# A gated transformer block on one core: the order of DMAs in an attention unit, and four smaller moves

## The chip, the cores and the metric

The kernel runs on one core of one Trainium2 chip. The metric is device time in microseconds (us) of one execution. Times of the kernel before are of three runs; the profile is of one more execution.

The engines are named as the profile names them: PE (TensorE, matmuls), DVE (VectorE), ACT (ScalarE), POOL (GpSimd) and SP (SyncE), which here only issues DMAs, in order, one queue for all of them.

## The reference, cut to what matters

The input `x` is 8 blocks of 128 rows by 512. Four layers are added to it, each behind a normalisation and times the tanh of a gate:

```
x = x + tanh(g_xattn[0]) * attention(layernorm(x), ctx, mask, position_bias, wq, wk, wv, w_out)
x = x + tanh(g_ffn[0])   * (layernorm(x) @ W4bit + f0_bias)
x = x + tanh(g_xattn[1]) * attention_one_head(layernorm(x), ctx, ...)
x = x + tanh(g_ffn[1])   * (layernorm(x) @ base_W.T + base_b + routed low-rank experts)
```

The first attention takes most of the time: 32 heads of 128, each over 8 blocks of 128 queries by 128 keys, with a bias for each head that all blocks share, a mask for each block, a softmax, the product with the values, and the output weights `w_out`, 128 rows of them for each head.

## The kernel before, in words

**Precision.** A product of two f32 matrices is done as three matmuls of high and low parts: each operand is split into a rounded part (`high`, by ACT) and the rest (`low`, by DVE or POOL), and the products high·high, high·low and low·high are summed in PSUM (`product`, L171, lines L177 to L179).

**Keys and queries (0 to some 310 us).** For a pair of heads, the 2x2 blocks of weights and context go through a scheme of seven products instead of eight (`seven`, L210). The first two pairs of keys are done plainly (`project_plainly`, L553): four PSUM banks, one for each head i and each half of the blocks, each summed over four row blocks of the context (two values of `inner`, two of `dc`). At the very start, SP loads the weights of head 0 (`wk_0`) and two blocks of the context, the weights of head 1 (`wk_1`) and two more, and then the other four blocks (L370 to L377). Keys and queries are stored to DRAM.

**Attention units (some 310 to 790 us).** A unit is one head and one half of the blocks; there are 64 (`unit`, L1005). In unit u of pair p, with r = u mod 4, are traced: two output products of a pair done before (`project_out`, L753, added into x on DVE by L750), value products (`make_values`, the next ones needed), the attention product `av` of unit u-4 (`attend`, L719), the sum of mask and position bias on POOL (`add_masks`, L651, instruction L657), the scores of unit u on PE (L669), their sum with mask and bias on DVE (L670), the negative maximum (L674), the transpose of the probabilities of unit u-3 on DVE (`transpose_probs`, L716, held behind that maximum), the exponentials on ACT (L684), and the normalising multiply on POOL (L692).

**The way through DRAM.** To transpose the probabilities, a unit stores them (`store_probs`, L700, tile `through`) and the next unit reads them back with four DMAs of 64 KB, each another block of 32 partitions (`move_probs`, L707, tile `moved`, two buffers). DVE then transposes within 32x32 blocks (L716, into `pT`), and PE uses `pT` in `av` (L731). One unit's chain is: scores, sum, maximum, exponentials, multiply, store, read, transpose, `av`.

**Loads of a unit.** `loads(u + 1)` (L992) is traced in unit u behind the store: queries and keys of unit u+4 (`fetch`, L580, DMAs L593), in two units of eight two blocks of value weights (`load_quad`, L281, tile `raw_wv`), the position bias of the next pair when the next unit has r = 3 (`load_bias`, L365), and a head's output weights when the next unit has r = 0 or 1 (`load_wo`, L281, tile `raw_wo`). The output weights are split into `wo_h` (ACT) and `wo_l` (POOL) in the units with r = 2 and 3 (`split_wo`, L354).

**What sets the order.** The program is traced in the order of the code; a planner then orders each engine's instructions by its own estimate of when each is ready, with earlier traced ones first. `behind(name)` (L139) holds what is traced within it behind a marked instruction on the same engine, without a semaphore. In the key and query stage and in the ending, PE keeps the traced order (`in_order`, L146); in the units the planner orders PE, too. Buffers are rotating slots with tags (L35): 4 of tag `s` (the scores of a unit, 256 KB), one of which the tile `cols` of small statistics holds (L736); 6 of tag `kq`, 7 of `raw`, 8 of `wo`.

**Ending (some 784 us on).** `ending` (L1338) does the last units' products, interleaved with the three later layers over the 8 blocks (`ffn0`, `xattn1`, `ffn1`). Before it, DVE multiplies the two biases of the later layers by their gates (L1067 into `bias0`, L1068 into `bb`); `add_row` (L1114) adds them to x on POOL.

Of the kernel before, what the change touches and what calls it, by code (L numbers as in the profile page):

```python
# [14 lines left out]
ALU = mybir.AluOpType  # L15
AX = mybir.AxisListType

P = 128
NB = 8
D = 512  # L20
NDC = D // P
H = 32
# [43 lines left out]
def kernel(  # L66
# [37 lines left out]
    nc = tc.nc  # L104
# [9 lines left out]
    def slot(shape, tag, name, dtype=F32):  # L114
        return sb.tile(shape, dtype, tag=tag, name=name, bufs=TAGS[tag])
# [6 lines left out]
    def wide_row(tag, name, dtype=F32):  # L122
        return slot([P, D], tag, name, dtype)
# [4 lines left out]
    def wide(t):  # L128

        return t.bitcast(F32)  # L130
# [4 lines left out]
    def mark(name, inst):  # L135
        marks[name] = inst.ins

    @contextmanager
    def behind(*names):  # L139
        with ExitStack() as stack:  # L140
            for name in names:
                stack.enter_context(tc.issue_after(marks[name]))
            yield
# [27 lines left out]
    def product(out, terms, start=True, stop=True, **more):  # L171


        n = len(terms)
        for i, ((lh, ll), (rh, rl)) in enumerate(terms):
            first, last = start and i == 0, stop and i == n - 1
            nc.tensor.matmul(out, lhsT=lh, rhs=rh, start=first, stop=False, **more)  # L177
            nc.tensor.matmul(out, lhsT=lh, rhs=rl, start=False, stop=False, **more)  # L178
            nc.tensor.matmul(out, lhsT=ll, rhs=rh, start=False, stop=last, **more)  # L179
# [6 lines left out]
    HK = NDC // 2  # L186
# [92 lines left out]
    def load(key, src, shape=(P, D)):  # L279
        t = slot(list(shape), "raw", f"raw_{key}")  # L280
        mark("load", nc.sync.dma_start(out=t, in_=src))  # L281
        raws[key] = t

    def load_pair(kind, p):
        if p < NP:
            w = {"wk": wk, "wq": wq}[kind]
            for h in (2 * p, 2 * p + 1):
                load(f"{kind}_{h}", w[:, h])
# [61 lines left out]
    def load_wo(h):  # L350
        if h < H:
            load(f"wo_{h}", wo[:, h])

    def split_wo(h):  # L354
        t = raws.pop(f"wo_{h}")
        high, low = (wide_row("wo", f"wo_{n}{h}", F32R) for n in "hl")
        split(high, low, t, nc.gpsimd)
        wos[h] = high, low
# [10 lines left out]
    cx_raw = {}  # L369
    for inner in range(2):  # L370
        for half in range(2):
            if inner == 0:
                load(f"wk_{half}", wk[:, half])
            for dc in range(inner * HK, inner * HK + HK):
                t = wide_row("wo", f"cxraw{half}{dc}")
                nc.sync.dma_start(out=t, in_=ctxT[:, dc, half * HALF * P : (half + 1) * HALF * P])
                cx_raw[half, dc] = t  # L377
    load_pair("wk", 1)
    lnw = wide_row("pT", "lnw")
    nc.sync.dma_start(out=lnw, in_=ln_w.partition_broadcast(P))  # L380
# [21 lines left out]
    tgx0, tgx1, tgf0, tgf1 = (tg[:, i : i + 1] for i in range(4))  # L402
# [150 lines left out]
    def project_plainly(kind, p, left, right):  # L553

        banks = {}

        turns = [(inner, half, i) for inner in range(2) for half in range(2) for i in range(2)]
        if p:
            turns.sort(key=lambda turn: (turn[1], turn[2], turn[0]))
        for inner, half, i in turns:  # L560
            if inner == 0:
                tag = ("mm", "av")[half]
                banks[i, half] = ptile([P, HALF * P], tag, f"c{i}{half}_{kind[0]}{p}")
            w, t = left[i], right[f"B{inner + 1}{half + 1}"]
            terms = [
                (
                    tuple(part[:, bass.ts(2 * inner + dc, P)] for part in w),
                    (t[:, 0, dc, :], t[:, 1, dc, :]),
                )
                for dc in range(HK)  # L570
            ]
            product(banks[i, half], terms, inner == 0, inner == 1)
            if inner:
                t = slot([P, HALF * P], "kq", f"{kind}{i}{half}_{p}")
                mark("copy", nc.scalar.copy(t, banks[i, half]))
                nc.sync.dma_start(out=stored[kind, p][:, 2 * i + half], in_=t)
# [126 lines left out]
    def move_probs(u):  # L703
        moved = slot([P, NQ, HALF, Q32], "moved", f"moved_{u}")
        blocks = probs[u].rearrange("(i q) n f -> n q i f", q=Q32)
        for j in range(NQ):
            move = nc.sync.dma_start(  # L707
                out=moved[bass.ts(j, Q32)].rearrange("p i b k -> p i (b k)"), in_=blocks[j]
            )
        mark("moved", move)  # L710
        probs[u] = moved
# [7 lines left out]
    def attend(u):  # L719
        h, half = where(u)  # L720
        p, i = divmod(h, 2)
        pT = probs.pop(u)
        if i == 0:
            attns[p, half] = page([P, 2, 2, HALF, P], f"a_{p}_{half}")
        a = attns[p, half][:, i]
        ah, al = a[:, 0], a[:, 1]
        cols = bass.ts(i, P)
        av = ptile([P, HALF, P], "av", f"av_{u}")
        for b in range(HALF):
            v = values_of[p, half, b // 2][:, b % 2, :]  # L730
            nc.tensor.matmul(av[:, b, :], lhsT=v[:, cols], rhs=pT[:, b, :], start=True, stop=True)  # L731
        mark("a", nc.scalar.copy(ah, av))  # L732
        mark("al", nc.vector.tensor_tensor(al, av, wide(ah), ALU.subtract))  # L733


    cols_all = slot([P, NB, 60], "s", "cols")  # L736
    places = {}

    def col(name, b, n=1):
        if name not in places:  # L740
            places[name] = sum(m for _, m in places.values()), n
        at, n = places[name]
        assert at + n <= 60
        return cols_all[:, b, at : at + n]

    def add_to_x(b, ps, factor, then=None):

# [151 lines left out]
    left = whole_pair(0)  # L899
# [61 lines left out]

    with in_order(*ORD):
        keys_and_queries()
    load_wo(0)

    last_keys = project(*order[-1], left, of_context)

# [24 lines left out]
    def loads(u):  # L992

        p, r = divmod(u, 4)
        n = u + (3 if u > FIRST - 4 else NU)
        if n >= FIRST:
            fetch(n)
        if u % 8 in (QUAD, QUAD + 1) and (u - QUAD) // 8 + 2 <= H // 4:
            load_quad((u - QUAD) // 8 + 2, (u % 8 - QUAD,))
        if r == 3:  # L1000
            load_bias(p + 1)
        if r in (0, 1):
            load_wo(2 * p + r)

    def unit(u):  # L1005
        p, r = divmod(u, 4)

        n = 2 * (u - OUT_LAG)

        goal = 14 + int(1.74 * (u - 3)) + min(AHEAD, u - 3, NU - 1 - u) if u > 3 else 0  # L1010
        if n >= 0:
            project_out(*divmod(n, NB))
        make_values((made + goal + 1) // 2)
        if u >= LAG:
            attend(u - LAG)
        if n >= 0:
            project_out(*divmod(n + 1, NB))
        make_values(goal)
        s = add_masks(u)
        for _ in range({0: 2, 1: 2, 2: 1, 3: 1, 4: 1}.get(u, 0)):  # L1020
            next(last_keys)
        scores(u, s)
        if u == NU - 1:
            move_probs(u - 1)
        store_probs(u)
        with behind("through"):
            loads(u + 1)
            if 0 < u < NU - 1:
                move_probs(u - 1)
        if r in (2, 3):  # L1030
            with behind("exp"):
                split_wo(2 * p + r - 2)

    make_values(7)
    unit(0)
# [18 lines left out]
    bias0 = load_row("bias0", f0_bias)  # L1054
    bq = load_row("bq", bq1)
    bb = load_row("bb", base_b)
# [6 lines left out]

    qkn = keep([P, NDC], "qkn")
    nc.vector.tensor_tensor(qkn, qnw, knw, ALU.mult)

    nc.vector.tensor_scalar(bias0, bias0, tgf0, None, ALU.mult)  # L1067
    nc.vector.tensor_scalar(bb, bb, tgf1, None, ALU.mult)  # L1068

    def transposed(b, name, src):  # L1070
        tag = "sc" if b % 2 and name in SC_NAMES else "av"
        tp = ptile([P, NDC, P], tag, f"tp{name}_{b}")
# [265 lines left out]
    def ending():  # L1338

        outs = iter(range(2 * (NU - OUT_LAG), NP * NB))  # L1340

        def project(n):
            for _ in range(n):
                project_out(*divmod(next(outs), NB))

        move_probs(NU - 1)
        with behind("moved"):
            for i in range(2):
                w_ffn.extend(load_page(f"wf{i}", ffn_kept[i]))
        make_values(made + 2)  # L1350
        project(2)
        attend(NU - 4)
        with behind("x"):
            transpose_probs(NU - 3)
        project(2)
        attend(NU - 3)
        project(1)
        yield
        project(3)
        with behind("x"):  # L1360
            transpose_probs(NU - 2)
        make_values(14 * (H // 4 + 1) - 2)
        attend(NU - 2)
        yield
        make_values(14 * (H // 4 + 1))
        transpose_probs(NU - 1)
        yield
        attend(NU - 1)
        project(4)
        yield  # L1370

    key, ffn, att, last = ([s(b) for b in range(NB)] for s in (keys, ffn0, xattn1, ffn1))
# [80 lines left out]
```

## Time and profile before

| what | us |
|---|---|
| median of three runs | 936.08 (935.97 to 937.21) |
| the profiled execution | 934.47 |
| its span | 932.7 |
| PE busy in it | 916.9 |
| DVE, ACT, POOL busy | 672.7, 503.4, 459.7 |

The span runs from the first to the last instruction of the program; the rest of the time lies around it. A busy PE is not PE at its peak, since the ends of matmuls are modelled; where PE loses time, its matmuls start further apart. Matmuls of 512 columns start some 0.23 us apart at full speed.

Issues by the page, with the median time to landing:

```profile
through<-s SPq DMA_DIRECT2D x64, 256.0 KB, 3.5
moved<-through SPq DMA_DIRECT2D x256, 64.0 KB, 3.8
q<-queries SPq DMA_DIRECT2D x58, 256.0 KB, 4.1
k<-keys SPq DMA_DIRECT2D x58, 256.0 KB, 4.8
```

A line gives the tile written and read, the queue, the count, the size of one, and the median us from issue to landing. In the answer on DMAs, those of `raw_wv` take 5.0 us, of `raw_wo` 5.1 and of the position bias 4.9.

### The profile page before, as it was taken

The numbers are of one execution on the slowest core, as the hardware profiler recorded it, in microseconds if no ns is written. First come the engines' busy times: TensorE is split into PE (matmuls) and PEld (weight loads), VectorE is DVE, ScalarE is ACT, GpSimd is POOL, SyncE is SP. The second block draws the span as 40 slices with busy tenths as digits, with TensorE's granted clock in tenths as the row PEclk, the third lists the DMA queues.
The fourth block names the chain that finished last, engine by engine and source line by source line (L and its number), as shares of the span: only waits on it lengthen the run. The fifth ranks groups of instructions, "written<-read, shape, count | busy, mean of one in ns | idle before, by whom it ended". The sixth has DMA issues, their size and how long they took to land.

```text
span 932.7 us, 16561 instructions
## 1 busy us (share of the span) xinstructions
PE 916.9 (98%) x5458; PEld 805.5 (86%) x5458; DVE 672.7 (72%) x1349; ACT 503.4 (54%) x1432; POOL 459.7 (49%) x513
## 2 busy tenths in 40 slices
PE   9999999999999998999999999999999999999998
PEld 7788888888888897999998889999998987888897
DVE  7887687888889676667676576766667667465686
ACT  6665465666645465445444444454545444577861
POOL 2455543133413445837567375673758733183441
PEclk9999999999999999999999999999999999999999
DMA  8665477889856928666665766666757566532001
GB/s 282 204 178 162 152 208 242 285 289 289 263 203 219 338 88 249 179 186 181 179 203 147 212 193 174 203 175 197 200 153 216 158 191 203 227 107 79 1 24 69
DMA packets 123909, 175.00 MB, mean 188 GB/s; under 512 B 16942, under 2 KB 52782, under 8 KB 122670
## 3 DMA queue, kind: packets, MB, share of 16 engines
q1 hardware_dynamic: 123822, 173.93, 61.5%
q8 instruction: 43, 0.70, 0.3%
q14 instruction: 44, 0.36, 0.1%
HBM read 109.85 MB, written 64.03 MB: 186 GB/s over the span
## 4 chain that ended last, share of the span: by engine, by line
PE 78%; DMA 7%; DVE 4%; ACT 4%; POOL 4%; issue 2%; SPq 2%; DVEq 0%; POOLq 0%; ACTq 0%
PE c_k L177 5%; PE pso L179 5%; PE c_k L178 5%; PE c_k L179 5%; PE pso L177 5%; PE c_q L177 5%; PE c_q L178 5%; PE c_q L179 5%; PE pso L178 5%; PE av L731 5%; PE c_v L177 5%; PE c_v L179 5%; PE c_v L178 5%; PE sc L669 4%; DMA moved<-through 3%
## 5 line engine op out<-in xcount | busy, mean ns | idle before, releaser
L684 ACT ACTIVATE s<-s,nm 128x128 f32<-128x128 f32 x256 | 99.8, 392 | 85.8 <-DVE nm L674 54.0
L750 DVE SCALAR_TENSOR_TENSOR x<-pso,tg,x 128x512 f32<-128x512 f32 x128 | 93.9, 738 | 47.5 <-PE pso L179 46.9
L692 POOL TENSOR_TENSOR s<-s,rs 128x512 f32<-128x512 f32 x64 | 66.8, 1044 | 85.9 <-DVE rs L690 65.6
L657 POOL TENSOR_TENSOR s<-mneg,bias 128x512 f32<-128x512 bf16 x64 | 75.8, 1190 | 65.8 <-DMA bias<-in_pbias_dram 23.9
L177 PE MATMUL pso<-wo_h,a 128*128 128x512 f32 x256 | 105.3, 413 | 1.2 <-DVE x L750 1.2
L179 PE MATMUL pso<-wo_h,a 128*128 128x512 f32 x256 | 105.6, 413 | 0.1
L178 PE MATMUL pso<-wo_l,a 128*128 128x512 f32 x256 | 101.1, 396 | 0.0
L732 ACT CAST a<-av 128x512 fp32r<-128x512 f32 x64 | 37.5, 585 | 96.0 <-PE av L731 96.0
L177 PE MATMUL c_v<-wvP,cxT 128*128 128x256 f32 x288 | 84.9, 295 | 0.6 <-ACT v L249 0.4
L179 PE MATMUL c_v<-wvP,cxT 128*128 128x256 f32 x288 | 81.4, 283 | 0.0
L178 PE MATMUL c_v<-wvP,cxT 128*128 128x256 f32 x288 | 81.3, 282 | 0.0
L731 PE MATMUL av<-pT,v 128*128 128x128 f32 x512 | 73.7, 278 | 5.4 <-DVE pT L716 5.4
L731 PEld LDWEIGHTS av<-pT,v 128*128 128x128 f32 x512 | 69.1, 192 | 10.8 <-DVE pT L716 6.6
L716 DVE STREAM_TRANSPOSE pT<-moved 128x512 f32<-128x512 f32 x64 | 45.0, 704 | 37.5 <-DMA moved<-through 37.5
L669 PEld LDWEIGHTS sc<-k,q 128*128 128x128 f32 x464 | 60.3, 191 | 4.9 <-DVE s L670 0.6
L669 PE MATMUL sc<-k,q 128*128 128x128 f32 x464 | 62.7, 275 | 0.4 <-DMA k<-keys 0.4
L177 PE MATMUL c_v<-wvP,cxB 128*128 128x256 f32 x216 | 62.0, 288 | 0.4 <-ACT v L264 0.4
L178 PE MATMUL c_v<-wvP,cxB 128*128 128x256 f32 x216 | 61.0, 282 | 0.0
L179 PE MATMUL c_v<-wvP,cxB 128*128 128x256 f32 x216 | 60.8, 282 | 0.0
L179 PEld LDWEIGHTS pso<-wo_h,a 128*128 128x128 f32 x256 | 48.6, 190 | 10.3 <-DVE a L733 1.3
L177 PEld LDWEIGHTS c_v<-wvP,cxT 128*128 128x128 f32 x288 | 54.8, 190 | 2.4 <-ACT wvP L168 0.7
L178 PEld LDWEIGHTS c_v<-wvP,cxT 128*128 128x128 f32 x288 | 54.8, 190 | 1.5
(281 smaller groups left out, 2801.2 us busy)
## 6 DMA issues: line engine op xcount, KB each, us to landing
keys<-keys SPq DMA_DIRECT2D x64, 256.0 KB, 3.6
queries<-queries SPq DMA_DIRECT2D x64, 256.0 KB, 3.7
through<-s SPq DMA_DIRECT2D x64, 256.0 KB, 3.5
moved<-through SPq DMA_DIRECT2D x256, 64.0 KB, 3.8
q<-queries SPq DMA_DIRECT2D x58, 256.0 KB, 4.1
k<-keys SPq DMA_DIRECT2D x58, 256.0 KB, 4.8
raw_wk<-in_wk_dram SPq DMA_DIRECT2D x32, 256.0 KB, 4.0
raw_wq<-in_wq_dram SPq DMA_DIRECT2D x32, 256.0 KB, 4.2
```

What stands on the lines that cost most here:

```text
L177: nc.tensor.matmul(out, lhsT=lh, rhs=rh, start=first, stop=False, **more)
L178: nc.tensor.matmul(out, lhsT=lh, rhs=rl, start=False, stop=False, **more)
L179: nc.tensor.matmul(out, lhsT=ll, rhs=rh, start=False, stop=last, **more)
L657: nc.gpsimd.tensor_tensor(s, mneg[:, half], bias.unsqueeze(2).to_broadcast([P, NQ, HALF, Q32]), ALU.add)
L669: nc.tensor.matmul(ps[:, j, :], lhsT=q[:, cols], rhs=k[:, cols], start=True, stop=True)
L684: e = nc.scalar.activation(one, one, AF.Exp, bias=nm[:, j : j + 1], accum_out=sm[:, j : j + 1])
L692: mark(f"norm{u}", nc.gpsimd.tensor_tensor(s, s, factors, ALU.mult))
L716: nc.vector.transpose(by_block(t), probs[u])
L731: nc.tensor.matmul(av[:, b, :], lhsT=v[:, cols], rhs=pT[:, b, :], start=True, stop=True)
L732: mark("a", nc.scalar.copy(ah, av))
L750: "x", nc.vector.scalar_tensor_tensor(xs[b], ps, factor, xs[b], ALU.mult, ALU.add, **out)
```

## The change

Five edits:

1. In a unit, the reads of the unit before (`move_probs`) come right behind the store, and the loads behind the reads (`behind("moved")`). Before, both were behind the store, the loads traced first.
2. The output weights of a pair are loaded one to two units later relative to their use (next unit r = 2 and 3 instead of 0 and 1 of the pair; the first one no longer ahead of the units) and split in the units with r = 3 and, of the next pair, r = 0. The last head's are split at the start of `ending`.
3. The tile `cols` is made when it is first used, in the ending, so that the units have four buffers of tag `s`.
4. The two gated biases are multiplied on DVE in the ending, behind `al` of unit 62.
5. The first two pairs of heads: for pair 0, the four banks are filled by one row block of the context at a time (both heads, then the next row block) and `wk_1` is loaded behind the first block instead of the second; in both pairs the three products of a term come in the order high·high, low·high, high·low, the low part of the weights first.

```diff
@@ loads at the start
-            if inner == 0:
-                load(f"wk_{half}", wk[:, half])
             for dc in range(inner * HK, inner * HK + HK):
+                if dc == half == 0:
+                    load("wk_0", wk[:, 0])
                 t = wide_row("wo", f"cxraw{half}{dc}")
                 nc.sync.dma_start(out=t, in_=ctxT[:, dc, half * HALF * P : (half + 1) * HALF * P])
                 cx_raw[half, dc] = t
+                if dc == half == 0:
+                    load("wk_1", wk[:, 1])
@@ project_plainly
-        turns = [(inner, half, i) for inner in range(2) for half in range(2) for i in range(2)]
+        turns = [
+            (*divmod(dc, HK), half, i)
+            for inner in range(2)
+            for half in range(2)
+            for dc in range(inner * HK, inner * HK + HK)
+            for i in range(2)
+        ]
         if p:
-            turns.sort(key=lambda turn: (turn[1], turn[2], turn[0]))
+            turns.sort(key=lambda turn: (turn[2], turn[3], turn[:2]))
...
+            nc.tensor.matmul(ps, lhsT=wh, rhs=th, start=first, stop=False)
+            nc.tensor.matmul(ps, lhsT=wl, rhs=th, start=False, stop=False)
+            nc.tensor.matmul(ps, lhsT=wh, rhs=tl, start=False, stop=last)
@@ the statistics' tile
-    cols_all = slot([P, NB, 60], "s", "cols")
+    cols_all = []
...
-        return cols_all[:, b, at : at + n]
+        if not cols_all:
+            cols_all.append(slot([P, NB, 60], "s", "cols"))
+        return cols_all[0][:, b, at : at + n]
@@ ahead of the units
-    load_wo(0)
@@ loads
-        if r in (0, 1):
-            load_wo(2 * p + r)
+        if r > 1:
+            load_wo(2 * p + r - 2)
@@ unit
         store_probs(u)
         with behind("through"):
-            loads(u + 1)
             if 0 < u < NU - 1:
                 move_probs(u - 1)
-        if r in (2, 3):
+        with behind("moved" if u else "through"):
+            loads(u + 1)
+        if r == 3 or r == 0 and p:
             with behind("exp"):
-                split_wo(2 * p + r - 2)
+                split_wo(2 * p if r else 2 * p - 1)
@@ ahead of the ending
-    nc.vector.tensor_scalar(bias0, bias0, tgf0, None, ALU.mult)
-    nc.vector.tensor_scalar(bb, bb, tgf1, None, ALU.mult)
@@ ending
+        with behind("exp"):
+            split_wo(H - 1)
         move_probs(NU - 1)
...
         attend(NU - 2)
+
+        with behind("al"):
+            nc.vector.tensor_scalar(bias0, bias0, tgf0, None, ALU.mult)
+            nc.vector.tensor_scalar(bb, bb, tgf1, None, ALU.mult)
```

More of the change, by code (lines that the diff above doesn't have):

```diff
@@ L555, in project_plainly @@
         banks = {}
-        turns = [(inner, half, i) for inner in range(2) for half in range(2) for i in range(2)]
+        turns = [
[5 more added lines that the diff above has]
+        ]
         if p:
-            turns.sort(key=lambda turn: (turn[1], turn[2], turn[0]))
-        for inner, half, i in turns:
-            if inner == 0:
+            turns.sort(key=lambda turn: (turn[2], turn[3], turn[:2]))
+        for inner, dc, half, i in turns:
+            first, last = inner + dc == 0, inner + dc == HK
+            if first:
                 tag = ("mm", "av")[half]
                 banks[i, half] = ptile([P, HALF * P], tag, f"c{i}{half}_{kind[0]}{p}")
[L564 to L573, printed above, removed]
+            wh, wl = (part[:, bass.ts(HK * inner + dc, P)] for part in left[i])
+            t = right[f"B{inner + 1}{half + 1}"]
+            th, tl = t[:, 0, dc, :], t[:, 1, dc, :]
+            ps = banks[i, half]
+            nc.tensor.matmul(ps, lhsT=wh, rhs=th, start=first, stop=False)
+            nc.tensor.matmul(ps, lhsT=wl, rhs=th, start=False, stop=False)
+            nc.tensor.matmul(ps, lhsT=wh, rhs=tl, start=False, stop=last)
+            if last:
                 t = slot([P, HALF * P], "kq", f"{kind}{i}{half}_{p}")
```

## The prediction

> **What bounds the kernel now.** I read the page's first part first, then who waits for whom on PE, then SP's queue in the stretch of the longest waits, then the chain there.
>
> ```profile
> span 932.7 us, 16561 instructions
> ...
> PE 916.9 (98%) x5458; PEld 805.5 (86%) x5458; DVE 672.7 (72%) x1349; ACT 503.4 (54%) x1432; POOL 459.7 (49%) x513
> ```
>
> TensorE (PE) is busy 98% of the span. The change removes no matmul (only the order of the first ones changes), so it can win only what PE loses between matmuls, and can lose any amount by making PE wait. The wait view of PE says what there is to win:
>
> ```profile
> PE av L731 <- DVE pT L716: 5.4, 6, 1.9
> PE pso L177 <- DVE x L750: 1.2, 2, 0.9
> PE c_k L177 <- ACT keys L242: 0.6, 1, 0.6
> PE sc L669 <- DMA k<-keys: 0.4, 1, 0.4
> ```
>
> The columns are total us, times, longest. The largest is the attention product `av` waiting for the transposed probabilities `pT`: 5.4 us at six places (362.19, 477.67, 517.18, 538.08, 710.12 and 762.79 us). DVE, which makes `pT`, waits itself in 20 of its 64 transposes, 37.5 us in all, for the read of the probabilities back from DRAM (`moved`). Only where that exceeds the slack does PE feel it. SP's queue shows why the reads are late:
>
> ```profile
> 527.92 0.34 SPq L700 DMA_DIRECT2D through<-s  x1
> 528.30 0.93 SPq L281 DMA_DIRECT2D raw_wv<-in_wv_dram  x2
> 529.28 0.43 SPq L281 DMA_DIRECT2D raw_wo<-in_wo_dram  x1
> 529.81 0.38 SPq L707 DMA_DIRECT2D moved<-through  x1
> 530.28 0.38 SPq L593 DMA_DIRECT2D q<-queries  x1
> 530.72 0.42 SPq L593 DMA_DIRECT2D k<-keys  x1
> 531.19 1.38 SPq L707 DMA_DIRECT2D moved<-through  x3
> ```
>
> The store of unit 27 goes out at 527.92, but one of the four reads of unit 26 stands behind three loads of 256 KB and the other three behind five. The last read starts at 532.14, 4.2 us behind the store, and lands 4.98 us later; DVE transposes at 537.31 and `av` starts at 538.08 after 1.89 us of idle PE. Over units 1 to 62 the last read starts 3.6 us behind its store on average (1.8 to 6.6). A second chain, at 460 us, starts elsewhere:
>
> ```profile
> 460.31 4.85 DMA bias<-in_pbias_dram
> ...
> 466.44 1.06 POOL s L692
> ...
> 467.51 0.34 SPq L700
> ...
> 471.71 5.00 DMA moved<-through
> ...
> 476.90 0.72 DVE pT L716
> 477.67 0.71 PE av L731 x4
> ```
>
> Every fourth unit, POOL's add of mask and bias (L657) waits 1.3 to 6.2 us for the bias load (65.8 us in 15 places; the page puts only part of it down to the bias, but all 15 are the units 4, 8, ... 60, whose bias is new); here the normalising multiply of the unit before (L692) stands behind it in POOL's order, and so do store, read, transpose and `av`. Keep this one in mind: the change moves that bias load.
>
> **The change, part by part.**
>
> *Store, reads, then loads.* The reads need nothing that is late: the store they read is a unit old, and their buffer was freed by a transpose ahead of the unit's exponentials. They now follow their store at once: 0.38 us, then four at 0.47 us, the last starting some 1.8 us after the store, against 3.6 now. So `pT` can come 1.9 us earlier on average, and over 2 us where loads of `wv` stand between. PE's losses, start to start (the wait view leaves out some 0.15 us of each as the pipeline's own), are 2.0 at 362, 0.5 at 477, 0.6 at 517, 2.05 at 538, 0.5 at 710 and 0.8 at 763. At 362 the last read of unit 2 starts 6.6 us behind its store: all goes, -2.0. At 477, 517, 538 and 710 the store itself will be 1.85 us later (next part). There the last read started 4.2, 4.9, 4.2 and 4.9 us behind; with 1.85 + 1.8 = 3.65 it still comes 0.5 to 1.2 us earlier, and nothing is queued before it in the DMA engines, where landing took 3.8 us in the median against 5.0 at the stalls. I take -0.5, 0, -1.7 and -0.4. Bounds for the five: none of 5.65, all of it.
>
> Right after the stall at 538, the `pso` matmuls stand 0.43 us apart in the chain (540.30 to 541.58) instead of 0.23, with the granted clock at 0.97 in the stretch from 476 to 544 where it is 1.00 elsewhere. That is four times 0.2 plus 0.3 on the one before: 1.1 us. I let it go with the stall: -1.1. For the stall as its cause stands that it begins 0.4 us after it; against, that the wait of 1.84 us at 362 has no such tail. [...]
>
> *What that pushes back.* Loads now start behind four reads, 1.85 us later. Queries and keys are fetched over two units ahead (15 us or more): hidden. The quads' `wv`: POOL has their low parts done 16 us or more before PE uses them, from the second quad on: hidden. The bias is not: its landing releases POOL's add in all of those 15 places. With it the scores' add on DVE comes later, then maximum, then the transpose of three units before, which stands behind that maximum. From the end of that transpose to its `av` there are 2.0 to 3.1 us in units 5, 9, ... 53, and 0.05 in unit 57, where PE already waits. A delay of 1.85 us is covered everywhere but there: +1.8. Bounds: 0 if the planner puts other work before the add, +13 at 3.5 us (a rival below).
>
> *`wo` loaded and split in other units.* 32 loads and 32 splits (ACT 0.6 us, POOL 1.3 us) as before, in other units; those of `wv` and `wo` no longer fall into the same ones. ACT and POOL stand at 54% and 49%. From load to split two units remain of three, some 14 us against a landing of 5.1. Not covered is the first pair: `wo` 0 and 1 were loaded at 316 and 324 and used from 352.6; now the second is issued near 349 and split after unit 4's exponentials, about 358. PE has value matmuls to fill with, but it loses 0.55 at 358 already. I take +0.5, between 0 and 2.5.
>
> *Gated biases.* DVE stands from 770.99 to 773.29: 0.83 waiting for the f0 bias, 1.55 multiplying it; 0.45 more for the other. PE's `pso` at 774.09 is 1.2 us late for the accumulation behind it. That goes: -1.2 (bounds -1.2 and 0). The same 0.9 to 2.0 us of DVE now stands at about 800.5, ahead of x's update with `psf` at 805.78; POOL's two adds of 0.72 come before that, done by 804: nothing.
>
> *Split of head 31 in the end.* Its load follows unit 62's store and reads, 2.3 us after 776.37, plus 4 to land, 0.6 and 1.3 to split: 784.6 at best; PE wants it about 0.7 us after 785.57. Margin 1.7; +0.3 (0 to 2).
>
> *The statistics tile made later* frees a fourth buffer for the scores. POOL waits before no add except those of the bias: nothing.
>
> *First head row block by row block.* Now PE does six matmuls by 8.19, then flows. After, `wk_1` lands where the second context block did (6.08) and the other way round, so six are done by then too; with the low weight ahead of the low context the second need not wait for DVE. The ninth starts at about 9.2 rather than 9.35: -0.2 (-0.4 to +0.4).
>
> Sum: -2.0 - 0.5 - 1.7 - 0.4 - 1.1 + 1.8 + 0.5 - 1.2 + 0.3 - 0.2 = -4.5. The profiled execution took 934.47 us with a span of 932.7, so 1.8 lie around it; that makes a span of 928.2 and a time of 930.0. The median of the three timed runs is 936.08, 1.6 above that execution; on the median, **931.6 us**.
>
> **Rivals.**
>
> *The bias decides, slower.* If the bias lands not 1.85 but 3.5 us later, the waits beyond the slack (3.04, 2.97 three times, 2.24, 2.15, 3.04, 3.05, 3.04, 3.05, 1.96, 2.64, 2.59, 0.05) sum to 13.2 us instead of 1.8: 943 us. It decides from a delay of about 2.95 us, where the waits eat all gains. For it: queries and keys stand ahead of the bias and can wait for buffers (a keys issue took 1.61 us at 401.97), and bias landings range from 4.5 to 6.2. Against it: scores free these buffers before the reads are through, and DVE loses fewer waits for `moved`. Chance 0.17.
>
> *DVE's order takes the place of the reads, no gain.* Before 44 of 64 transposes DVE did not wait at all: they come when their turn comes. If the planner, with other landing times, places them later, `av` waits as long as now, and only the gated biases and the head are won: -0.6, 935.5. Chance 0.16. That the change doesn't do what it says is part of this: in 6 of 62 units the reads already follow within 0.6 us.
>
> [...] Chance 0.12.
>
> *All stalls go*, the bias costing nothing: 1.8 + 0.5 + 0.3 more, and the rest of the five waits (1.05): 928.0. Chance 0.12.
>
> The forecast itself: 0.43. The range 927.5 to 938 holds all but the bias case and the edges. A measurement of this kernel tells about 0.2% (1.9 us) from no change: below 934.2 lie the forecast, the dip and all-stalls-go, 0.67; within, 0.16, the case of DVE's order; above, 0.17, the bias case.
>
> **What would show it.** Reads standing right behind each store in SP's queue; DVE's wait for `moved` well below 37.5 us; PE's wait for `pT` at 1 to 3 us with its largest piece near 763; the bias about 1.85 us later against its store and POOL's wait for it at 80 to 95 us; no wait of PE at 774; no half clock near 540. I am wrong if `av` waits in many units 4k+1 (bias case), or if `pT` comes as late as now with reads landed early (DVE's order).

## The result, and the profile after

The changed kernel takes 927.38 us (median of six runs, 925.86 to 928.90), beside 936.03 us for six runs of the kernel before (934.20 to 944.21): a ratio of 0.9894, 95% interval 0.9858 to 0.9931. That is 8.7 us less by the medians (9.9 by the ratio) where 4.5 were forecast, and 0.1 us under the low end of the range. Ratios, here and below, are to the kernel before on the same chip and are worked out from all runs but the disturbed ones, so the ratio of two medians can stand a little apart from them.

The profiled execution took 925.86 us with a span of 924.0. First the page's first lines:

```profile
span 924.0 us, 16542 instructions
...
PE 913.0 (99%) x5458; PEld 804.3 (87%) x5458; DVE 676.4 (73%) x1349; ACT 504.9 (55%) x1432; POOL 459.4 (50%) x513
```

PE does the same 5458 matmuls, is busy 3.9 us less than before and idle 4.8 us less. What PE waits for (line waited at, releaser: total us, times, longest):

```profile
PE sc L677 <- DVE s L678: 1.8, 1, 1.8
PE pso L177 <- ACT a L740: 1.4, 2, 1.1
...
PE av L739 <- DVE pT L724: 0.2, 1, 0.2
```

The wait of `av` for `pT`, 5.4 us at six places before, is down to 0.2 at one. A wait that was not among the large ones has come: the scores of unit 5, at 356.11, wait 1.8 us for DVE's add of unit 4. The reads in SP's queue stand where the change puts them:

```profile
522.11 0.33 SPq L708 DMA_DIRECT2D through<-s  x1
522.53 1.83 SPq L715 DMA_DIRECT2D moved<-through  x4
524.70 0.34 SPq L601 DMA_DIRECT2D q<-queries  x1
525.08 0.43 SPq L601 DMA_DIRECT2D k<-keys  x1
```

All four reads now follow the store, and the loads come after them. From the page's groups and its list of issues, the add of mask and bias on POOL (x count | busy, mean ns | idle before it) and the reads (count, size, median us to landing):

```profile
L665 POOL TENSOR_TENSOR s<-mneg,bias 128x512 f32<-128x512 bf16 x64 | 75.3, 1186 | 35.5 <-DMA bias<-in_pbias_dram 14.3
...
moved<-through SPq DMA_DIRECT2D x256, 64.0 KB, 2.8
```

The reads land a microsecond faster than before (3.8). The first line is the one to stop at. The bias is issued 4.0 us behind its store, where it was 1.5 before; so POOL should wait longer for it, and I had forecast 80 to 95 us. It waits 35.5, against 65.8 before. The bias also lands faster, some 4.3 us after its issue against 4.9, but that makes up only a quarter of the 2.5 us. A later operand and a shorter wait then go together only if POOL comes to the add later, having done something else first.

**What POOL does first.** Here is POOL before the change, around the bias of unit 20 (start, us, line, what, count, and in brackets the idle time ahead of it):

```profile
457.90 1.04 POOL L692 TENSOR_TENSOR s<-s,rs 128x512 f32<-128x512 f32 x1 [4.22 <-DVE rs L690]
458.90 1.29 POOL L169 TENSOR_TENSOR wo_l<-raw_wo,wo_h 128x512 fp32r<-128x512 f32 x1
465.32 1.17 POOL L657 TENSOR_TENSOR s<-mneg,bias 128x512 f32<-128x512 bf16 x1 [5.13 <-DMA bias<-in_pbias_dram]
466.44 1.05 POOL L692 TENSOR_TENSOR s<-s,rs 128x512 f32<-128x512 f32 x1
```

and DVE there, which makes the factors of the multiply at L692:

```profile
461.88 0.16 DVE L690 TENSOR_TENSOR rs<-rs,anykey 128x4 f32<-128x4 f32 x1
```

The factors of unit 19 are there at 462.04. The multiply starts at 466.44, 4.4 us later, because the add of unit 20 stands ahead of it and waits 5.13 us for a bias. Its store goes out at 467.51, and behind that store in SP's queue are the reads of unit 18, whose `av` is the stall of 0.5 us at 477.67. With its factors there, the multiply did not pass the waiting add.

After the change, the same multiply starts 0.15 us after its factors, which end at 463.54, and the add comes two instructions later, 0.14 us after the bias lands at 469.61 (the profile names another DMA as what it waited for last):

```profile
463.69 1.04 POOL L700 TENSOR_TENSOR s<-s,rs 128x512 f32<-128x512 f32 x1 [5.16 <-DVE rs L698]
466.02 1.28 POOL L169 TENSOR_TENSOR wo_l<-raw_wo,wo_h 128x512 fp32r<-128x512 f32 x1 [1.29 <-ACT wo_h L168]
469.75 2.30 POOL L665 TENSOR_TENSOR s<-mneg,bias 128x512 f32<-128x512 bf16 x2 [2.45 <-DMA raw_wo<-in_wo_dram]
```

I read this order from the trace for all 15 units that have a new bias. Before, the add stood ahead of the multiply in 9 of the 15, and the 15 multiplies started 44.4 us in all after their factors. After, it stands ahead in 1 of 15, with 5.7 us in all. No line of the change says so. The likely reason, which no run shows directly, is that the loads are now traced behind the reads: the planner then reckons with a later bias, and its order puts the multiply first. In e7 below, where the bias is loaded early again, the add is ahead again in 12 of 15.

### The profile page after: what moved, and what is told of

Read it like the earlier page. It is cut to its first block, busy times and chain, and to the rows that moved or that the text cites. A ratio compares the mean times of both kernels' runs of the same rounds, so it can differ in the third digit from the quotient of the medians.

```text
span 924.0 us, 16542 instructions
## 1 busy us (share of the span) xinstructions
PE 913.0 (99%) x5458; PEld 804.3 (87%) x5458; DVE 676.4 (73%) x1349; ACT 504.9 (55%) x1432; POOL 459.4 (50%) x513
## 4 chain that ended last, share of the span: by engine, by line
PE 83%; ACT 4%; DVE 3%; DMA 3%; POOL 2%; issue 1%; SPq 1%; DVEq 0%; POOLq 0%; ACTq 0%
PE pso L177 6%; PE pso L179 6%; PE pso L178 6%; PE av L739 6%; PE c_v L177 6%; PE sc L677 6%; PE c_v L179 6%; PE c_v L178 6%; PE c_q L177 5%; PE c_q L179 5%; PE c_q L178 5%; PE c_k L177 4%; PE c_k L179 4%; PE c_k L178 4%; DMA raw_wv<-in_wv_dram 2%; ACT h L1103 1%
## 5 line engine op out<-in xcount | busy, mean ns | idle before, releaser
L692 ACT ACTIVATE s<-s,nm 128x128 f32<-128x128 f32 x256 | 99.8, 392 | 101.3 <-DVE nm L682 76.5
L665 POOL TENSOR_TENSOR s<-mneg,bias 128x512 f32<-128x512 bf16 x64 | 75.3, 1186 | 35.5 <-DMA bias<-in_pbias_dram 14.3
L739 PE MATMUL av<-pT,v 128*128 128x128 f32 x512 | 71.2, 275 | 0.2 <-DVE pT L724 0.2
L739 PEld LDWEIGHTS av<-pT,v 128*128 128x128 f32 x512 | 66.3, 192 | 2.4 <-DVE pT L724 0.4
L678 DVE TENSOR_TENSOR s<-sc,s 128x512 f32<-128x512 f32 x64 | 43.7, 683 | 27.2 <-POOL s L665 22.5
L177 PEld LDWEIGHTS c_v<-wvP,cxT 128*128 128x128 f32 x288 | 54.7, 190 | 2.8 <-ACT wvP L168 0.7
L741 DVE TENSOR_TENSOR a<-av,a 128x512 fp32r<-128x512 f32 x64 | 43.5, 679 | 18.2 <-ACT a L740 17.7
```

The source lines that it names most:

```text
L665: nc.gpsimd.tensor_tensor(s, mneg[:, half], bias.unsqueeze(2).to_broadcast([P, NQ, HALF, Q32]), ALU.add)
L678: nc.vector.tensor_tensor(s, by_block(ps), s, ALU.add)
L692: e = nc.scalar.activation(one, one, AF.Exp, bias=nm[:, j : j + 1], accum_out=sm[:, j : j + 1])
```

## The experiments

The theory after the result was that POOL's order is what the steady units gained from. The rivals were the reads' place in SP's queue, and the other edits. In the table, "add first" counts the units of 15 in which POOL's add stands ahead of the multiply; "late" is the sum over these 15 of multiply start less end of its factors; "idle" is POOL's idle time before the adds, from the page; "PE loss" adds up, from 380 us to the last `av`, what each matmul starts later than is usual for its pair of widths (30th percentile), where that is over 0.15 us. Times are medians of all runs.

| kernel | us | ratio, 95% interval | add first | late | idle | PE loss |
|---|---|---|---|---|---|---|
| before | 936.03 | 1 | 9 | 44.4 | 65.8 | 9.2 |
| changed | 927.38 | 0.9894 (0.9858 to 0.9931) | 1 | 5.7 | 35.5 | 1.5 |
| e1, edit 1 alone | 932.99 | 0.9960 (0.9938 to 0.9982) | 0 | 6.0 | 43.6 | 7.6 |
| e2, all but edit 1 | 935.63 | 0.9970 (0.9948 to 0.9992) | 9 | 21.7 | 50.5 | 8.6 |
| e3, edit 4 alone | 936.38 | 1.0008 (0.9982 to 1.0033) | 9 | 44.7 | 64.6 | 8.4 |
| e4, edit 2 alone | 938.83 | 1.0002 (0.9974 to 1.0031) | 9 | 22.3 | 50.7 | 8.7 |
| e9, edits 1 and 2 | 928.55 | 0.9905 (0.9877 to 0.9933) | 1 | 6.0 | 33.9 | 2.5 |
| e6, all but edit 3 | 926.45 | 0.9893 (0.9862 to 0.9924) | 1 | 6.1 | 32.3 | 1.7 |
| e8, before and one line | 927.26 | 0.9889 (0.9862 to 0.9917) | 0 | 3.7 | 39.5 | 2.3 |
| e7, changed, bias first | 926.21 | 0.9876 (0.9848 to 0.9904) | 12 | 15.6 | 62.5 | 1.2 |
| e11, changed, add held first | 932.52 | 0.9941 (0.9920 to 0.9962) | 15 | 83.3 | 59.6 | 3.5 |
| e13, all but edit 1, and the line | 928.93 | 0.9904 (0.9871 to 0.9937) | 0 | 3.1 | 17.5 | 4.8 |
| e12, changed, bias first and the line | 926.83 | 0.9886 (0.9851 to 0.9920) | 0 | 3.5 | 3.4 | 0.9 |
| e14, edit 1, bias first and the line | 924.69 | 0.9873 (0.9856 to 0.9889) | 0 | 5.2 | 3.1 | 0.9 |
| e15, e12 without edit 2 | 922.51 | 0.9854 (0.9832 to 0.9877) | 0 | 6.4 | 3.5 | 0.9 |
| e16, changed, beside e15 | 928.08 | 0.9909 (0.9887 to 0.9931) | 1 | 5.8 | 33.1 | 2.2 |

### The edits by themselves

e1 is the kernel before with the first edit:

```diff
         with behind("through"):
-            loads(u + 1)
             if 0 < u < NU - 1:
                 move_probs(u - 1)
+        with behind("moved" if u else "through"):
+            loads(u + 1)
```

> The kernel before with edit 1 alone: the reads right behind the store, the loads behind the reads. Theory 1 (the reads' place in SP's queue is what PE waited for, and the planner now puts the normalising multiply ahead of the add that waits for the bias, so the later bias costs nothing in the steady units): PE's wait for pT falls from 5.4 to under 1 us, the half clock near 540 goes, and it is 5 to 7 us faster than before; the stall at 774 stays. Rival (the moved output weights and the other edits carry it, by taking five-load queues apart): 0 to 3 us faster.

e2 is the changed kernel with that edit undone (the same lines the other way).

> The changed kernel with edit 1 undone: loads and reads both behind the store, the loads traced first. Theory 1: it loses most of the gain, 1 to 3 us faster than before, with 3 us or more of waiting for pT. Rival (the other edits carry it): 5 us or more faster than before.

e3 has the fourth edit alone, e4 the second alone:

```diff
-    nc.vector.tensor_scalar(bias0, bias0, tgf0, None, ALU.mult)
-    nc.vector.tensor_scalar(bb, bb, tgf1, None, ALU.mult)
...
         attend(NU - 2)
+        with behind("al"):
+            nc.vector.tensor_scalar(bias0, bias0, tgf0, None, ALU.mult)
+            nc.vector.tensor_scalar(bb, bb, tgf1, None, ALU.mult)
```

> The kernel before with edit 4 alone: the two gated biases multiplied in the ending. The prediction's step: 1.2 us faster, no wait of PE for x near 774, nothing lost in the ending. Rival (DVE's other work near 774 is as late without them): 0.3 us or less.

```diff
-    load_wo(0)
...
-        if r in (0, 1):
-            load_wo(2 * p + r)
+        if r > 1:
+            load_wo(2 * p + r - 2)
...
-        if r in (2, 3):
+        if r == 3 or r == 0 and p:
             with behind("exp"):
-                split_wo(2 * p + r - 2)
+                split_wo(2 * p if r else 2 * p - 1)
...
+        with behind("exp"):
+            split_wo(H - 1)
```

> The kernel before with edit 2 alone: output weights loaded and split in other units. The prediction's step: 0.5 us slower by the first pair and 0.3 by the last head. Rival (fewer loads stand ahead of the reads in the units with value weights, so the reads come earlier even without edit 1): 2 to 4 us faster, PE's wait for pT under 3 us.

The first edit gains 0.40% alone, less than half of the whole; all the others together gain 0.30%; the gated biases and the output weights alone gain nothing that can be told. So the gain is not a sum of edits. e4 says why, and also limits the theory: with the output weights elsewhere the multiplies' lateness halves (22.3), yet PE loses as much. Lateness alone is no price; it counts where it exceeds the slack.

The first edit was expected to gain 5 to 7 us and gained 3.7 by the ratio. In e1 the multiply comes first on POOL in all 15 units and PE still loses 7.6 us. The chain of waits near one of its stalls (start, us, what):

```profile
434.06 1.25 POOL wo_l L169
435.31 3.75 issue
439.09 1.18 POOL s L657
440.29 0.70 DVE s L670
441.02 0.04 DVE nm L674
...
441.62 0.71 DVE pT L716
442.33 0.04 issue
442.37 1.16 PE av L731 x8
```

and POOL's row of the same add:

```profile
439.09 2.28 POOL L657 TENSOR_TENSOR s<-mneg,bias 128x512 f32<-128x512 bf16 x2 [3.78 <-DMA bias<-in_pbias_dram]
```

This is the chain that I had forecast as the cost of a late bias: add, scores' add, maximum, transpose of three units before, `av`. The stalled `av` at 442.4 and 500.8 are those of units 13 and 21, of the form 4k+1, as forecast; at 441.0, 499.5 and 558.6 scores wait just behind such late adds. The longest stall is of another kind: PE waits 1.80 us at 572.14 for `pT` of unit 31, and DVE there waited for its reads:

```profile
571.37 0.71 DVE L716 STREAM_TRANSPOSE pT<-moved 128x512 f32<-128x512 f32 x1 [2.63 <-DMA moved<-through]
```

So the first edit does two things that work against each other.

### Edits 1 and 2 together, and all but edit 3

e9 is e1 and e4 in one; e6 is the changed kernel with the statistics' tile made early, as before:

```diff
-    cols_all = []
+    cols_all = slot([P, NB, 60], "s", "cols")
...
```

> The kernel before with edits 1 and 2: the reads right behind the store, and output weights in other units. Theory 1 (the two belong together: edit 1 alone made the bias late and put the fourth units' stalls in the place of the old ones, edit 2 takes POOL's and SP's extra work out of those units): 7 to 9 us faster than before, PE losing under 3 us in the steady units. Rival (each is worth its own part): 3.5 to 5 us faster, as edit 1 alone, 933.

> The changed kernel with the statistics tile made early again, so that the units have three buffers for scores. The prediction's step: nothing, within 1 us of the changed kernel. Rival (the fourth buffer lets POOL's add go ahead of a store that has not landed, now that the store is on every unit's critical part): 2 us or more slower than the changed kernel, with POOL waiting before the add for a store in units other than 4k.

Edits 1 and 2 are nearly the whole change (928.55). Beside edit 1 the second edit gains 4.4 us by the medians, which are of two chips (5.1 by the ratios). Part of what it does can be seen: from the end of the transposes of units 5, 9, ... 57 to their `av` lie 2.3 us on average in e9 and 1.3 in e1, so a microsecond more slack is left. The tile (926.45 without it) pays nothing, as forecast.

### One line in place of the change

e8 is the kernel before with the add of units 4k held behind the multiply of unit 4k-1 instead of 4k-2:

```diff
-        with behind(*(f"norm{u - 2}",) * (u > 1)):
+        back = 2 if u % 4 else 1
+        with behind(*(f"norm{u - back}",) * (u > 1)):
```

> The kernel before with one line more: in the units whose bias is new, POOL's add of mask and bias stands behind the normalising multiply of the unit before instead of two before, so that no multiply waits for the bias. Theory 1 (half of the loss of before was this: the stalls at 477 and 538 hang on a multiply behind the bias wait): 2 to 4 us faster than before, the stalls at 477 and 538 gone, that at 362 left. Rival (the reads' place in the queue alone made them): within 1 us of before.

It takes 927.26 us, as much as the changed kernel: some 10 us less than before by the ratio, where 2 to 4 were expected. The reads are as late as before (3.6 us behind their store on average, the last of them). POOL at the same bias of unit 20, and the factors from DVE:

```profile
459.74 1.29 POOL L169 TENSOR_TENSOR wo_l<-raw_wo,wo_h 128x512 fp32r<-128x512 f32 x1
462.95 1.04 POOL L693 TENSOR_TENSOR s<-s,rs 128x512 f32<-128x512 f32 x1 [1.92 <-ACT wo_h L168]
466.23 2.30 POOL L658 TENSOR_TENSOR s<-mneg,bias 128x512 f32<-128x512 bf16 x2 [2.24 <-DMA bias<-in_pbias_dram]
```

```profile
462.64 0.16 DVE L691 TENSOR_TENSOR rs<-rs,anykey 128x4 f32<-128x4 f32 x1
```

The multiply starts 0.15 us after its factors (462.80) instead of 4.4, and the store of unit 19 with it; the add still waits 2.24 us for the bias, now with nothing ready behind it. The stalls at 477, 538, 710 and 763 are gone; the one at 362 stays (1.59 us at 362.52), as expected.

### The order forced back

e11 is the changed kernel with the multiply of units 4k-1 held behind the add of 4k:

```diff
...
+        mark("mask", added)
...
+        if u % 4 == 3 and u < NU - 1:
+            early_masks[u + 1] = add_masks(u + 1)
+        with behind(*("mask",) * (u % 4 == 3 and u < NU - 1)):
-        mark(f"norm{u}", nc.gpsimd.tensor_tensor(s, s, factors, ALU.mult))
+            mark(f"norm{u}", nc.gpsimd.tensor_tensor(s, s, factors, ALU.mult))
...
```

> The changed kernel with one order forced back: in the units 4k-1 POOL's normalising multiply is held behind the mask's add of unit 4k, which waits for the bias to land. The reads still stand right behind the unit's store in SP's queue, as the change put them. Theory (what the change gained is POOL's order: in before, 9 of these 15 multiplies stood behind an add that waited for its bias, 44 us of lateness in all; in the changed kernel 1 of 15): all 15 multiplies now wait for a bias that also lands later than in before, PE's wait for pT comes back, and the time is 4 to 8 us above the changed kernel's, 931 to 935 us. Rival (the gain is the reads' place in SP's queue): the reads are as early as in the changed kernel, so the time stays within 1.5 us of it, 926 to 929 us.

```profile
459.10 1.04 POOL L706 TENSOR_TENSOR s<-s,rs 128x512 f32<-128x512 f32 x1 [0.17 <-DVE rs L701]
468.00 1.17 POOL L665 TENSOR_TENSOR s<-mneg,bias 128x512 f32<-128x512 bf16 x1 [7.87 <-DMA bias<-in_pbias_dram]
469.13 1.04 POOL L706 TENSOR_TENSOR s<-s,rs 128x512 f32<-128x512 f32 x1
```

932.52 us: the theory's range. But its detail did not come true. PE's waits for `pT` did not come back in the steady units (1.6 us at one place, 361.4); the multiplies are 83 us late in all, and PE loses only 3.5 us there, against 9.2 in the kernel before and 1.5 in the changed kernel. Another 2.4 us more than in the changed kernel lie between 345 and 380 us, at the start of the units. So, beside the other edits, early reads take most of the steady loss away even with every multiply late, just as e8's order takes it away with late reads. Either of the two is enough for most of it; e2 has the late reads and 21.7 us of lateness, and keeps 8.6. The rival is wrong as the only cause and right as a second one.

### The line without the first edit

e13 is e2 and the line of e8.

> All of the change but the first edit (the bias and the reads stay where before had them in SP's queue), and the add of unit 4k held behind the multiply of unit 4k-1. Without that last line the same kernel took 935.6 us. Theory (the first edit acted only by making the planner put the multiply first): the one line stands in for the edit, and the time is that of the changed kernel, 925.5 to 928 us. Rival (the reads' place gives a part of its own, which the other edits need): 930 to 935.6 us.

928.93 us beside 935.6 without the line (on two chips; 0.9904 against 0.9970): the line stands in for the first edit, to within the interval. The time is 0.9 us over the theory's range, and PE's loss of 4.8 us shows that early reads have a little left to give.

### The bias first

e7 is the changed kernel with the position bias loaded right behind the store, ahead of the reads; e12 adds the line of e8.

```diff
-        if r == 3:
-            load_bias(p + 1)
...
         with behind("through"):
+            if (u + 1) % 4 == 3:
+                load_bias(p + 1)
             if 0 < u < NU - 1:
                 move_probs(u - 1)
```

> The changed kernel with the position bias loaded ahead of the reads, right behind the store; everything else behind them as in the change. Theory 1 (the bias's delay costs what is left, above all the 2.0 us of PE at 356, unit 4): 1.5 to 2.5 us faster than the changed kernel, POOL's wait for the bias under 15 us. Rival (PE's early loss is slack that the later units need: what is won at 356 is lost again further on): within 1 us of the changed kernel, with new waits for pT or scores after 380.

> The changed kernel with the bias loaded right behind the store, ahead of the unit's reads, and the add of unit 4k held behind the multiply of unit 4k-1. Theory: with POOL's order fixed by hand, the earlier bias can no longer pull the add ahead of the multiply (it did in 12 of 15 units when only the bias was moved), and it lands before the multiply is done, so the stalls that the late bias makes (2.0 us at unit 4) go as well: 924 to 926.5 us, 1 to 3 us below the changed kernel. Rival (the stall of unit 4 only moves on to the next late operand, as it did to 359.8 when only the bias was moved): 926 to 928 us, within 1 us of the changed kernel.

Neither can be told from the changed kernel (e7's theory had been 1.5 to 2.5 us, with POOL's wait under 15). In e7 the earlier bias pulls the add ahead of the multiply again (12 of 15), late by 15.6 us in all, which the early reads cover. In e12 POOL's idle time before the adds is 3.4 us and PE loses 0.9 us in the steady units; what it wins there it loses at the start, where the scores wait 3.64 us for keys at 360.17. The rival (the stall moves on to the next late operand) was right.

e14 puts the same two into e1, that is, edit 1 without its late bias:

> The kernel before with the first edit alone, but the bias loaded right behind the store, ahead of the reads, and the add of unit 4k held behind the multiply of unit 4k-1. The first edit alone took 933.0 us although every multiply stood ahead of the add; its stalls lay at units whose add came late. Theory (there the later bias took back what the order on POOL gave): with the bias some 2 us earlier and the same order on POOL the stalls at 441, 499.5, 558.6, 572 and 739.8 us go, and the time is that of the one-line kernel (927.3 us), 926 to 929 us. Rival (the bias was not the cause, but POOL, where the splits of the output weights and of the quads' value weights fall into the same units as long as the second edit is left out): 931 to 934 us.

924.69 us, 1.3 us under the theory's range, 8.1 us less than e1 by the ratios. None of e1's stalls behind 380 us is left, and PE loses 0.9 us there instead of 7.6. So the later bias was the loss in e1, and the clash on POOL was not: the splits fall into the same units in both, and the multiply stood ahead of the add in all 15 units of e1 already.

### The best version

e15 is e12 with the second edit undone, and e16 is the changed kernel beside it.

> The changed kernel without its second edit (the output weights are loaded and split where before had them), with the bias loaded right behind the store, ahead of the reads, and the add of unit 4k held behind the multiply of unit 4k-1. With the second edit in, the same kernel took 926.8 us; the first edit alone with the same two lines took 924.7 us. Theory (the second edit helps only while the bias is late; with that mended it pays nothing and may cost at the start of the units, where a wait of 3.8 us for keys stood at 360.2): 923 to 925.5 us, 2 to 4 us below the changed kernel beside it. Rival (the second edit is neutral, and 926.8 against 924.7 is the spread between chips): within 1 us of the changed kernel.

> The changed kernel as it is, beside the version without its second edit on the same chip. Both theories: 925 to 929 us; it is there so that a difference of 2 us is read on one chip.

922.51 us (922.14 to 923.88) against 928.08 (926.44 to 929.24) on one chip: 5.6 us faster than the changed kernel, 1.5% faster than the kernel before, and 0.5 us under the theory's low end; 2 to 4 us below the changed kernel were expected. Its page and POOL at the bias of unit 20:

```profile
span 920.3 us, 16543 instructions
...
L666 POOL TENSOR_TENSOR s<-mneg,bias 128x512 f32<-128x512 bf16 x64 | 75.2, 1186 | 3.5 <-DMA bias<-in_pbias_dram 3.5
```

```profile
459.77 1.04 POOL L701 TENSOR_TENSOR s<-s,rs 128x512 f32<-128x512 f32 x1 [2.89 <-ACT wo_h L168]
460.77 2.30 POOL L666 TENSOR_TENSOR s<-mneg,bias 128x512 f32<-128x512 bf16 x2
```

The add follows the multiply without a wait, and two adds are done by 463.1 where before the first began at 465.3. With the bias early, the second edit no longer gains; by the ratios it costs 3 us (e12 against e15, on two chips, with intervals that overlap), and in the profiles that lies at the start of the units, where e12 waits 3.64 us for keys and e15 0.9 us. The keys land only 0.7 us apart (360.04 and 359.35). The rest is PE's order: e15 has a block of value products and an `av` ahead of those scores, from 356.0 to 358.5, and in e12 those value products stand behind them, from 361.87. Why the order differs is not settled.

## Why the prediction was wrong, point by point

The direction and the stage were right; the size was half, and the first edit, on which most of the forecast rested, brings less than half of the whole gain without the second. **The step that failed is "What that pushes back"**, the term +1.8 for the later bias. It took POOL's order as it stood (add, then multiply) and only moved the add's operand. Its lower bound, "0 if the planner puts other work before the add", names what happened and prices it wrongly: the work put first is the multiply, which had stood up to 5.9 us late behind the add. The profile had shown this chain (460 to 478 us, quoted in the prediction), and I read it as a cost of a late bias, not as an order that a later bias could undo. Three of the stalls I counted (477, 538 and 710, units 18, 26 and 50) have reads behind the store of a unit 4k-1 whose multiply was 4.4 to 5.1 us late; I put them down to the loads ahead of the reads. e8 removes them with the loads in place. Two readings behind those terms were off as well: the last read started 3.4 us behind its store at 517 and 4.3 at 710, not 4.9. Without the +1.8 the sum would have been -6.3.

PE's loss by stage (as in the table, over 0.15 us each), against the terms of the sum:

| stage | before | after | forecast | measured |
|---|---|---|---|---|
| start, to 300 us | 4.2 | 4.1 | -0.2 | -0.1 |
| first `av` and 35 us on | 3.6 | 4.1 | -2.0 + 0.5 | +0.5 |
| steady units, to the last `av` | 9.2 | 1.5 | -0.5 - 1.7 - 0.4 - 1.1 - 1.2 + 1.8 + 0.3 | -7.6 |
| ending | 3.4 | 3.0 | none | -0.4 |
| spacing under 0.15 us | 28.4 | 27.2 | none | -1.2 |

With 300 to 345 us unchanged (0.4), these make the 8.7 us of the spans (932.7 to 924.0). The steady units came out 4.8 us better than forecast and the first `av` and what follows 2.0 us worse, so errors of opposite sign partly cancel in the total.

- **Early stall, -2.0.** The stall at 362 went, and one of the same length came at 356: the scores of unit 5 wait for DVE's add of unit 4, and that waits for POOL's add of the new bias:

```profile
349.43 0.43 SPq L365 DMA_DIRECT2D bias<-in_pbias_dram  x1
```

```profile
355.36 0.69 DVE L678 TENSOR_TENSOR s<-sc,s 128x512 f32<-128x512 f32 x1 [4.77 <-POOL s L665]
```

  The bias is issued at 349.43 and lands at 354.04, POOL's add starts at 354.18 and DVE's at 355.36. I had costed the later bias from unit 5's `av` on only; here it cost 2.0 us at another engine's wait. That the bias makes this stall was not tried by itself: in e7, with the bias first, the wait moved to 359.8, for keys. A wait of 1.1 us came at 376.81 too, where `pso` waits for ACT's `a`; I did not follow it further.
- **Steady stalls, -0.5, -1.7, -0.4, and the half clock, -1.1.** All went, and 517 and 763 (1.4 us), held at nothing, as well. No half clock follows: the granted clock is 1.00 from 538 to 542, where it was 0.62 and 0.52 before; that the dip stays had been given 0.12.
- **The bias, +1.8.** It is issued 2.5 us later, not 1.85, and the stall at unit 57 that it should have lengthened is gone: 1.9 us of slack lie there between transpose and `av` where 0.05 lay. The mechanism itself exists: with the bias early and the order on POOL held, e1 becomes 8 us faster by the ratios (e14).
- **Output weights, +0.5 (0 to 2.5), and head 31, +0.3.** Alone nothing can be told (1.0002, 0.9974 to 1.0031). I gave the edit a price of its own; its worth hangs on the bias: -4.4 us beside edit 1; with the bias early it looks like +3, from two chips whose intervals overlap.
- **Gated biases, -1.2.** The stall at 774 is gone in the trace, of e3 too. In time, e3's interval (-1.7 to +3.1 us) cannot tell -1.2 from nothing.
- **Tile, 0.** Right (e6). **First head, -0.2.** The first stage shows -0.1; it was not run alone.

Of the rivals, "all stalls go" (928.0) came nearest, but for a reason that I had not given: the bias did not come to cost nothing, it was traded for POOL's order. The "bias decides" rival had the right mechanism and the wrong company. What would have shown me wrong was on the list: 35.5 us of POOL's wait where I had 80 to 95.

## What to carry to other kernels

Look at what stands ready behind a waiting instruction on its engine before you ask how to shorten the wait: here a multiply stood 4.4 us behind an add that waited for its bias, and one line of order (e8) was worth as much as five edits. When a planner orders by estimated times, moving a load can change the order of the engine that uses it too (here POOL's add stood first in 9 of 15 units before, in 1 with the loads later and in 12 with the bias early again), so read that engine's order again, not its wait alone. And a change whose parts push against each other is worth undoing part by part after it has won: without one of its edits, with the load that it delayed put first and with the line of e8, it gained another 5.6 us (e15).

## What the runs showed that was not expected

The granted clock fell to half around one wait of PE of 1.89 us, and not around another of 1.84. Before, around the wait of 1.89 us that ended at 538.08 (the stretch; busy us of PE, PEld, DVE, ACT, POOL; then granted clock, DMA share, GB/s):

```profile
536.00:538.00 2.00, 0.19 (x2) 0.00 (x0) 0.69 (x2) 0.00 (x0) 0.00 (x0) 1.00 0.86 244
538.00:540.00 2.00, 1.92 (x10) 1.82 (x10) 1.96 (x6) 0.00 (x0) 0.98 (x1) 0.62 0.96 354
540.00:542.00 2.00, 2.00 (x7) 1.61 (x7) 0.93 (x2) 1.10 (x2) 2.00 (x3) 0.52 1.04 293
542.00:544.00 2.00, 2.00 (x12) 1.65 (x11) 1.44 (x3) 0.62 (x1) 2.00 (x3) 1.00 0.51 142
```

From 538.50 to 541.91, 3.41 us, the clock is 0.50. The changed kernel, around its wait of 1.84 us that ended at 356.11:

```profile
354.00:356.00 2.00, 0.26 (x2) 0.00 (x0) 0.64 (x1) 0.00 (x0) 1.82 (x2) 1.00 0.90 280
356.00:358.00 2.00, 1.89 (x16) 1.89 (x17) 1.94 (x4) 1.05 (x5) 0.45 (x1) 1.00 0.79 199
```

Nearly the same wait, and no fall; nor behind the wait of 1.84 us at 362 in the kernel before (1.00 from 362 to 366). The other runs do not sort by length either. The clock fell around a wait of 2.10 us in e9 (ended at 357.70; 0.57 from 358 to 360, 0.58 from 360 to 362) and around one of 3.64 us in e12 (ended at 360.17; 0.62, 0.50, 0.50 and 0.67 in the four stretches of 2 us from 358). In e8, behind a wait of 1.59 us, seven `av` matmuls took 1.86 us, where seven took 1.05 behind the wait at 362; the mean granted clock of that execution is 0.998. In e1 and e13, with waits of 1.80 and 1.99 us, it is 1.0. So the length of a wait alone does not decide in these runs. What does was not shown.
